# A fused four-layer decoder: values weighed ahead of the next unit's scores, and ones matmuls ahead of the last norm's transposes in the local blocks

## The chip, the cores and the metric

The kernel runs on one core of a Trainium2 chip. The metric is the time of one execution on the device in microseconds (us); lower is better. The engines are TensorE (PE in the profile, with its weight loads as PEld), VectorE (DVE), ScalarE (ACT), GpSimd (POOL) and SyncE (SP).

## The reference

A decoder of four layers, in float32, on x of 16 sequences x 64 tokens x 128 features, with a context of the same shape. Every layer has a self-attention or a recurrence, a cross attention and a feed-forward part, each with a residual and a layer norm after it. What this change touches lies in layer 0's third part, a small stack of two local-attention layers:

```python
for l in range(2):
    h = shift_token(x)                    # second half of the features from the token before
    q, k, v = split(h @ wqkv[l])          # 8 heads of 64
    q, k = rotary_xpos(l2norm(q) * qs, l2norm(k) * ks)
    attn = softmax(where(mask, -max, 8 * q @ k.T))     # causal, inside a window of 64 tokens
    x = x + (attn @ v) @ wo
    h = layer_norm(shift_token(x)) * lg + lb
    a, g = split(h @ w1 + b1)
    x = x + (a * gelu(g)) @ w2 + b2
x = layer_norm(x_before + x)
```

A sequence has 64 tokens, so a window is a sequence. What follows the stack is layer 1's self-attention (at1) and its cross attention (xa1).

## The kernel before, in words

The 1024 tokens are cut into two halves of 512, h = 0 and h = 1. Each half is a Python generator (`first_stream`) that emits one step of work up to each `yield`; `side_by_side` takes a step of half 0, then a step of half 1, and so on, with half 0 five steps ahead. Every engine carries out its instructions in the order that comes out of this, after a scheduler has moved some of them by a few places. [...]

`local_half(h)` emits the two local layers of one half. A half has two units u of 256 tokens, a unit two rows r of 128 tokens. One layer has these helpers:

- `rotate(u)`: the q and k products (lb_qk), their norms on ACT and DVE, and the rotary turn (lb_t; the sums on POOL).
- `values(u)`: the v products (lb_pv), copied to lb_v with a column of ones for the softmax sums.
- `flip(u)`: transposes of q and k (lb_pf, L868), copied to lb_qkT.
- `weights(u)`: 32 score matmuls, listed as 64 in the profile, into lb_sc (L880), two more for the mask (L889), the maximum (L901) and the subtraction (L902) on DVE, and Exp on ACT (L905), which gives lb_e.
- `turn(u)`: transposes of lb_e (lb_pt, L914), copied to lb_eT.
- `weigh(u)`: for each row 32 matmuls of lb_eT by lb_v into two PSUM tiles lb_av (L932), the reciprocal of the sum column (L942) and the product with it (L943, lb_ao). At the end of row 1 it calls `gather(u, 0)`.
- `gather(u, r)`: transposes of lb_ao (lb_pao, L957), copied to lb_oT (L958).
- `put(u)`: the output product (lb_po) and the residual (L972).

Then come the layer's norm (lb_hn), its transposes (lb_phn) behind six ones matmuls, the gated products (lb_pg, lb_pa, Gelu on ACT at L1045, the gating product on DVE at L1048), and the second product (lb_pw) with the residual (L1063 in layer 0, L1068 in layer 1). Layer 0 ends with transposes (lb_px) and their copies to lb_hs, which the next layer's lb_qk reads. Layer 1 ends in `close`, with the tag "lb": statistics on DVE, the inverse root on POOL, the normed xt_lb on DVE (L206). Its `flip`, called one step later, transposes xt_lb (px_lb, L224), and ACT copies that to x_lb, which at1's q and k products (at_pq, at_pk) read.

The order of the steps before the change, for each layer:

```python
            turn(0)
            flip(1)
            yield
            weights(1)
            weigh(0)
            yield
            turn(1)
            gather(0, 1)
            put(0)
```

With half 0 five steps ahead and eleven steps to a layer, `weights(1)` and `weigh(0)` of a half stand between the gated products of the other half and its lb_pw. In half 0's first layer they stand beside the end of half 1's first cross attention (xa_pao, po_xa, y_xa, px_xa).

`keep_busy` is one matmul of 128x128 ones by 128x512 ones in bfloat16 (L156, "ones"); its result is overwritten. at1 and the cross attentions place such matmuls in front of many of their products. `close` has a parameter `ones`, the number of them that its `flip` places ahead of the transposes; it is 0 unless given, and the local block gave none.

PSUM tiles of the pool `pt` (all of lb_pf, lb_pg, lb_pa, lb_pt, lb_av, lb_pao, lb_po, lb_pw and the like) rotate through four buffers: a tile waits for the readers of the tile four places earlier. lb_sc and lb_qk are of another pool with two. SBUF tiles of one size, lb_e, lb_eT, lb_oT and lb_t among them, rotate through seven buffers.

Of the kernel before, what the change touches and what calls it, by code (L numbers as in the profile page):

```python
# [37 lines left out]
class Kernel:  # L38
# [745 lines left out]
    def local_half(self, h):  # L784

        nc = self.nc
        work, psc, pt = self.aw, self.psc, self.pt
# [3 lines left out]
        for l in range(2):  # L791
# [64 lines left out]
            def flip(u):  # L856

                to = self.buf(8, [8, 256], f"{tag}_qkT{u}")
                both, rs = turned.pop(u)
                for r, t1 in enumerate(both):  # L860
                    t3 = t1.rearrange("p t (n d) -> p (t n) d", d=64)
                    nc.gpsimd.tensor_tensor(  # L862
                        t3, t3, rs[:, bass.ts(r, 16)].unsqueeze(2).to_broadcast([P, 16, 64]), ALU.mult
                    )
                    for t in range(2):
                        ps = pt.tile([P, 4, P], F32, tag="t", name=f"{tag}_pf{u}{r}{t}")
                        for c in range(4):
                            nc.tensor.transpose(ps[:, c, :], t1[:, t, bass.ts(c, P)], ident)  # L868
                        nc.scalar.copy(to[:, 4 * t : 4 * t + 4, bass.ts(r, P)], ps)
                qkT[u] = to  # L870

            def weights(u):
                sc = psc.tile([P, 2, HALF], F32, tag="sc", name=f"{tag}_sc{u}")
                for r in range(2):
                    for c in range(4):
                        for j in range(2):
                            for hh in range(2):
                                rows = slice(64 * hh, 64 * hh + 64)
                                t = slice(r * P + 64 * j, r * P + 64 * j + 64)
                                nc.tensor.matmul(  # L880
                                    sc[64 * j : 64 * j + 64, hh, bass.ts(r * 4 + c, S)],
                                    qkT[u][rows, c, t],
                                    qkT[u][rows, 4 + c, t],
                                    start=r == 0 and c == 0,
                                    stop=False,
                                    skip_group_check=True,
                                )
                for hh in range(2):
                    nc.tensor.matmul(  # L889
                        sc[:, hh, :],  # L890
                        self.ident_b,
                        self.causal_b.unsqueeze(1).to_broadcast([P, 8, S]),
                        start=False,
                        stop=True,
                        skip_group_check=True,
                    )
                e = self.buf(4, [2, 4, P], f"{tag}_e{u}")
                e3 = e.rearrange("p g n (a k) -> p (g n a) k", k=S)
                scored = sc.rearrange("p g (n k) -> p (g n) k", k=S)
                mx = work.tile([P, 16], F32, tag="mx", name=f"{tag}_mx{u}")  # L900
                nc.vector.tensor_reduce(mx, scored, AX.X, ALU.max)  # L901
                nc.vector.tensor_tensor(  # L902
                    e3, scored, mx.unsqueeze(2).to_broadcast([P, 16, S]), ALU.subtract
                )
                nc.scalar.activation(e3, e3, AF.Exp, scale=8.0)  # L905
                es[u] = e
# [11 lines left out]
            def weigh(u):  # L918


                eT = eTs.pop(u)
                oTs[u] = self.buf(4, [2, 4, P], f"{tag}_oT{u}")
                for r in range(2):
                    av = [
                        pt.tile([P, 4, 65], F32, tag="t", name=f"{tag}_av{u}{r}{cp}") for cp in range(2)
                    ]
                    for a in range(2):
                        for hh in range(2):
                            for j in range(2):
                                for cp in range(2):  # L930
                                    rows = slice(64 * cp, 64 * cp + 64)
                                    nc.tensor.matmul(  # L932
                                        av[cp][64 * j : 64 * j + 64, 2 * a + hh, :],
                                        eT[rows, hh, r * 2 + a, 64 * j : 64 * j + 64],
                                        v[rows, u * 4 + r * 2 + j, 2 * a + hh, :],
                                        start=True,
                                        stop=True,
                                    )
                    ao = self.buf(2, [2, 4, 64], f"{tag}_ao{u}{r}")
                    for cp in range(2):  # L940
                        rc = work.tile([P, 4], F32, tag="rc", name=f"{tag}_rc{u}{r}{cp}")
                        nc.vector.reciprocal(rc, av[cp][:, :, 64])  # L942
                        nc.vector.tensor_tensor(  # L943
                            ao[:, cp, :, :],
                            av[cp][:, :, 0:64],
                            rc.unsqueeze(2).to_broadcast([P, 4, 64]),
                            ALU.mult,
                        )
                    aos[u, r] = ao.rearrange("p c n d -> p (c n d)")
                    if r == 1:  # L950
                        gather(u, 0)

            def gather(u, r):
                flat = aos.pop((u, r))
                ps = pt.tile([P, 4, P], F32, tag="t", name=f"{tag}_pao{u}{r}")
                for n in range(4):
                    nc.tensor.transpose(ps[:, n, :], flat[:, bass.ts(n, P)], ident)  # L957
                nc.scalar.copy(oTs[u][:, r, :, :], ps)  # L958
# [29 lines left out]
            turn(0)  # L988
            flip(1)
            yield  # L990
            weights(1)
            weigh(0)
            yield
            turn(1)
            gather(0, 1)
# [65 lines left out]
            if l == 0:  # L1061
                x_in = self.buf(2, [4, D], f"{tag}_x2")
                nc.vector.tensor_tensor(x_in, ps, base, ALU.add)  # L1063
                self.shifted(self.psum(pt, f"{tag}_px"), h, x_in)
                yield
            else:
                y = self.new_y("lb", h)
                nc.vector.tensor_tensor(y, ps, base, ALU.add)  # L1068
                flip = self.close(pt, h, y, "lb")
                yield "last"  # L1070
                flip()

# [922 lines left out]
```

## Time and profile before

| | us |
|---|---|
| three runs | 893.00, 896.45, 899.19 |
| median | 896.45 |
| profiled execution | 892.14 |
| its span | 890.4 |
| PE busy | 737.5 (83%) |
| DVE busy | 493.2 (55%) |
| ACT busy | 361.7 (41%) |
| POOL busy | 264.8 (30%) |

The mean granted clock of PE in the profiled execution is 0.893 of full speed. The local blocks of the two halves lie between about 113 and 372 us of the span. [...] In a row of the timeline the columns are start, duration, engine, line, operation, what is written from what, shapes, count, and in brackets the idle time before it with what ended it. In a row of the chain they are start, duration, engine, tile and line. In a row for a stretch they are the bounds, the length, busy time and count of PE, PEld, DVE, ACT and POOL, the granted PE clock, the DMA share and GB/s.

### The profile page before, as it was taken

How to read it: one execution, taken by the hardware profiler on the slowest of the kernel's cores; microseconds unless marked ns; L12 is line 12 of the kernel's file. 1: busy time of each engine (PE TensorE's matmuls, PEld its weight loads, DVE VectorE, ACT ScalarE, POOL GpSimd, SP SyncE). 2: the span in 40 equal slices, each digit the busy share in tenths (PEclk: the TensorE clock that was granted, in tenths of full speed). 3: DMA queues.
4: the chain of work that ended last, by engine and by line, in shares of the span. 5: the costliest groups of instructions: out<-in, count | busy, mean ns of one | idle time of the engine just before them, and what ended most of it. 6: DMA issues, size and time to landing. Idle time of an engine off the chain costs nothing.

```text
span 890.4 us, 17664 instructions
## 1 busy us (share of the span) xinstructions
PE 737.5 (83%) x7145; PEld 467.7 (53%) x7147; DVE 493.2 (55%) x1126; ACT 361.7 (41%) x602; POOL 264.8 (30%) x299
## 2 busy tenths in 40 slices
PE   6777888878777889789978999869767999968990
PEld 2334546455554556457564577536444565735770
DVE  4565466564846656364536575445444456665663
ACT  2223456355455534364713365323215434512320
POOL 2323143260615321212025300146151011017732
PEclk7878989899999999899977899969968799968995
DMA  7700000000000000500000000152106632021102
GB/s 278 242 13 13 1 1 2 13 1 2 1 1 1 2 1 1 190 2 1 1 1 1 1 3 1 43 134 71 49 22 190 190 115 76 14 107 51 54 25 80
DMA packets 35543, 44.43 MB, mean 50 GB/s; under 512 B 7732, under 2 KB 27445, under 8 KB 34824
## 3 DMA queue, kind: packets, MB, share of 16 engines
q1 hardware_dynamic: 33000, 38.26, 13.6%
q0 software_dynamic: 2464, 5.05, 2.0%
q8 instruction: 58, 0.95, 0.4%
q14 instruction: 21, 0.17, 0.1%
HBM read 34.51 MB, written 11.80 MB: 52 GB/s over the span
## 4 chain that ended last, share of the span: by engine, by line
PE 54%; DVE 18%; POOL 7%; ACT 5%; issue 4%; DMA 3%; SPq 1%; DVEq 0%; POOLq 0%; ACTq 0%
PE xa_sc L480 4%; PE xa_av L572 4%; PE xa_pt L551 3%; PE tt_py L151 3%; PE sw_pe L151 3%; PE tt_ph L151 2%; PE at_sc L480 2%; DVE lb_t L818 2%; PE lb_qk L151 2%; DVE lb_t L832 2%; PE at_av L572 2%; PE xa_sc L491 2%; PE at_pt L551 2%; PE xa_pt L156 1%; PE lb_pw L151 1%
## 5 line engine op out<-in xcount | busy, mean ns | idle before, releaser
L536 DVE TENSOR_REDUCE xa_mx<-xa_sc 128x16 f32<-128x1024 f32 x40 | 48.7, 1219 | 63.8 <-PE xa_sc L491 41.3
L838 POOL TENSOR_TENSOR lb_t<-lb_t,lb_t 128x1024 f32<-128x1024 f32 x16 | 37.7, 2357 | 99.4 <-DVE lb_t L832 95.2
L554 ACT COPY xa_eT<-xa_pt 128x512 f32<-128x512 f32 x80 | 45.5, 587 | 40.8 <-PE xa_pt L551 40.0
L540 ACT ACTIVATE xa_e<-xa_e 128x1024 f32<-128x1024 f32 x40 | 42.3, 1058 | 37.6 <-DVE xa_e L537 37.5
L480 PE MATMUL xa_sc<-xa_km,xa_q 32*64 32x256 f32 x640 | 55.2, 404 | 0.7 <-ACT xa_q L431 0.5
L441 POOL TENSOR_SCALAR xa_km<-xa_k,const 128x512 f32<-128x512 f32 x40 | 27.0, 695 | 82.5 <-ACT xa_k L429 49.1
L551 PE MATMUL xa_pt<-const,xa_e 128*128 128x128 f32 x320 | 48.8, 280 | 1.8 <-ACT xa_e L540 1.8
L537 DVE TENSOR_TENSOR xa_e<-xa_sc,xa_mx 128x1024 f32<-128x1024 f32 x40 | 48.7, 1218 | 2.1
L551 PEld LDWEIGHTS xa_pt<-const,xa_e 128*128 128x128 f32 x320 | 40.3, 145 | 13.1 <-ACT xa_e L540 3.7
L572 PEld LDWEIGHTS xa_av<-v,xa_eT 128*64 128x64 f32 x1280 | 40.5, 138 | 8.2 <-issue 6.1
L572 PE MATMUL xa_av<-v,xa_eT 128*64 128x18 f32 (+1 forms) x1280 | 44.2, 209 | 0.0
L156 PEld LDWEIGHTS <-ones_b 128*128 128x128 bf16 x255 | 25.3, 106 | 35.9 <-issue 19.8
L151 PE MATMUL lb_qk<-w,lb_hs 128*128 128x512 f32 x64 | 35.8, 686 | 8.5 <-DVE lb_t L832 4.8
L480 PEld LDWEIGHTS xa_sc<-xa_km,xa_q 32*64 32x64 f32 x640 | 24.7, 136 | 19.9 <-issue 12.8
L201 POOL TENSOR_TENSOR rstd_xa<-mv_xa,eps 128x4 f32<-128x4 f32 x8 | 1.6, 200 | 112.2 <-DVE mv_xa L197 112.2
L814 DVE TENSOR_REDUCE lb_ss<-lb_t 128x16 f32<-128x1024 f32 x16 | 19.5, 1217 | 27.9 <-ACT lb_t L811 27.9
L156 PE MATMUL xa_pt<-ones_b 128*128 128x512 bf16 x80 | 30.2, 390 | 0.0
L862 POOL TENSOR_TENSOR lb_t<-lb_t,lb_rs 128x1024 f32<-128x1024 f32 x16 | 30.1, 1902 | 0.0
L1610 POOL DMA_INDIRECT tt_out<-tt_ys,tt_outs x23 | 22.5, 976 | 18.6 <-DVE tt_ys L1609 16.2
L868 PE MATMUL lb_pf<-const,lb_t 128*128 128x128 f32 x128 | 20.1, 312 | 9.4 <-POOL lb_t L862 9.3
L480 PE MATMUL at_sc<-at_km,at_q 32*64 32x256 f32 x256 | 22.5, 446 | 6.0 <-DVE at_rel L533 4.5
L151 PE MATMUL sw_pe<-sw_gu,sw_xs 128*128 x46 | 26.7, 665 | 0.0
(471 smaller groups left out, 1762.9 us busy)
## 6 DMA issues: line engine op xcount, KB each, us to landing
sw_gu<-in_sw_gu SPq DMA_DIRECT2D x4, 1024.0 KB, 6.8
at_mem<-at_rsb SPq DMA_DIRECT2D x16, 256.0 KB, 2.7
at_rel<-at_mem SPq DMA_DIRECT2D x32, 128.0 KB, 2.9
w<-in_w SPq DMA_DIRECT2D x1, 3114.0 KB, 13.7
sw_dn<-in_sw_dn SPq DMA_DIRECT2D x4, 512.0 KB, 7.0
tt_w<-in_tt_w SPq DMA_DIRECT2D x2, 1024.0 KB, 8.0
tt_b<-in_tt_b SPq DMA_DIRECT2D x1, 2048.0 KB, 7.4
sw_in<-in_zeros SPq DMA_DIRECT2D x1, 1472.0 KB, 11.2
```

What stands on the lines that cost most here:

```text
L151: self.nc.tensor.matmul(out, lhsT, rhs, start=n == 0, stop=n == len(pairs) - 1)
L156: self.nc.tensor.matmul(out, self.ones_b, self.ones_b.unsqueeze(1).to_broadcast([P, 4, P]), start=True, stop=True)
L441: nc.gpsimd.tensor_scalar(kms[-1][:, i % 4, :], k, hm[:, i : i + 1], 1.0, ALU.mult, ALU.mult)
L480: nc.tensor.matmul(sc[64 * j : 64 * j + 64, gg, at : at + 256], q[r, t], part[r, :, t] if local else part[r, :, :], start=not masked or (p ...
L536: nc.vector.tensor_reduce(mx, scored, AX.X, ALU.max)
L537: nc.vector.tensor_tensor(e3, scored, mx.unsqueeze(2).to_broadcast([P, 16, S]), ALU.subtract)
L540: nc.scalar.activation(e3, e3, AF.Exp, scale=scale)
L551: nc.tensor.transpose(ps[:, bass.ts(n, P)], blocks[:, bass.ts(n, P)], self.g("ident"))
L554: nc.scalar.copy(eT[:, gg, :], ps)
L572: nc.tensor.matmul(av[64 * j : 64 * j + 64, pr, hp, :, :], eT[:, gg, at : at + 64], v[:, b, hp, :, :], start=True, stop=True,)
L838: nc.gpsimd.tensor_tensor(t1, t1, t2.rearrange("p t n d -> p t (n d)"), ALU.add)
L862: nc.gpsimd.tensor_tensor(t3, t3, rs[:, bass.ts(r, 16)].unsqueeze(2).to_broadcast([P, 16, 64]), ALU.mult)
```

## The change

In each local layer `weigh(0)` is emitted ahead of `weights(1)`, within the same step. The close of the local block gets ones: 2 matmuls for half 0 and 7 for half 1, between the last lb_pw and the transposes px_lb.

```diff
             turn(0)
             flip(1)
             yield
+            weigh(0)
             weights(1)
-            weigh(0)
             yield
             turn(1)
             gather(0, 1)
@@
                 y = self.new_y("lb", h)
                 nc.vector.tensor_tensor(y, ps, base, ALU.add)
-                flip = self.close(pt, h, y, "lb")
+                flip = self.close(pt, h, y, "lb", ones=2 + 5 * h)
                 yield "last"
                 flip()
```

In the instruction order that results, PE has for each layer the lb_av matmuls, the four lb_pao transposes of row 0, and then the scores with the mask, where it had the scores first. DVE has the four reciprocals and four products ahead of the maximum and the subtraction. ACT has the copy lb_oT of row 0 ahead of the Exp. POOL and SP keep their order. Beside half 1's close the 7 ones stand behind the last at_av of half 0's attention, then the two ones of at_pq and at_pk, then the four px_lb transposes together, which were interleaved with those two ones.

## The prediction

> **What bounds the kernel now.** I read the page's shares first, then the chain of waits from 140 to 225 us and from 360 to 382, then the timeline of the same stretches with its releasers, and last the busy time and granted clock of single stretches. The page says that TensorE (PE) is 54% of the chain and that its clock is not full throughout:
>
> ```profile
> PE 54%; DVE 18%; POOL 7%; ACT 5%; issue 4%; DMA 3%; SPq 1%; DVEq 0%; POOLq 0%; ACTq 0%
> PEclk7878989899999999899977899969968799968995
> ```
>
> The reordered steps run four times: at about 149 us (call it A: half 0, layer 0, beside the end of half 1's first cross attention), 204 (B: half 1, layer 0), 256 (C: half 0, layer 1) and 310 (D: half 1, layer 1). B, in the chain of waits:
>
> ```profile
> 204.46 1.09 PE lb_sc L880 x64
> 205.55 0.55 PE lb_sc L889 x2
> 206.10 0.02 issue
> 206.13 1.23 DVE lb_mx L901
> 207.35 0.09 DVE lb_rc L942
> 207.44 1.17 DVE lb_e L902
> 208.61 0.33 DVE lb_ao L943
> ...
> 209.59 0.44 PE lb_pao L957 x2
> 210.04 2.69 PE lb_pw L151 x24
> ...
> 213.57 0.66 PE lb_px L235 x4
> 214.22 0.87 PE lb_pt L914 x8
> ```
>
> and in the timeline:
>
> ```profile
> 206.02 1.16 PE L932 MATMUL lb_av<-lb_v,lb_eT 64*64 64x65 f32 x64
> 208.69 1.28 ACT L905 ACT_TABLE_LOAD   x1 [4.37 <-DVE lb_e L902]
> 209.09 0.95 PE L957 MATMUL lb_pao<-const,lb_ao 128*128 128x128 f32 x4 [1.91 <-DVE lb_rc L942]
> ```
>
> The reader is to see that PE ends the value products at 207.18 and stands still until 209.09: their quotients (lb_ao) are queued on VectorE behind the maximum and the subtraction of the other unit's scores, and everything after on PE, the other half's lb_pw first, stands behind lb_pao. Also that ScalarE's table load for Exp waits for lb_e. C has the same rows 51.8 us later, D 105.9 later.
>
> The second edit is at half 1's close:
>
> ```profile
> 368.46 0.76 DVE xt_lb L206
> 369.26 0.47 PE px_lb L224
> 369.74 0.43 PE at_pq L156
> ...
> 371.91 2.07 PE at_pq L151 x2
> 373.98 1.72 PE at_pk L151 x2
> 365.60:369.20 3.60, 0.04 (x2) 0.00 (x0) 2.40 (x12) 0.00 (x0) 1.92 (x3) 0.95 0.94 292
> 369.00:375.60 6.60, 5.66 (x10) 2.22 (x10) 2.70 (x12) 1.17 (x2) 2.61 (x4) 0.50 0.98 361
> ```
>
> The last two lines are stretches: PE works 0.04 us of 3.6, and then has a clock of 0.50 for 6.6 us. Half 0's at_pq at 324.20, at full clock, takes 1.12 us for the same two matmuls.
>
> [...] the half clock comes in spells of 3.4 us or twice that (164.0 to 167.4, 369.0 to 375.6), behind idle stretches. [...] lb_ao waits behind lb_e with its operands long there. [...] the trace has 1283 ns for all six at L905.
>
> **The move, part by part.** It adds no work; PE, VectorE and ScalarE keep their instructions in another order, POOL and SP keep theirs. B, starting when lb_sc started (204.46):
> 1. The 64 lb_av matmuls (1.16) go first. Tiles rotate through four PSUM buffers, and the last of the four lb_av tiles takes the buffer that half 0's third gating multiplication (L1048, 204.57 to 205.32) reads. So the second 32 matmuls start at 205.36: end 205.9. This is the added wait; before, the scores covered it.
> 2. VectorE, nothing in front now: two reciprocals 0.20, two products 0.36 each (spacing at 175.86 to 176.66) from 205.32: 206.24. Last two lb_pao transposes: 206.5.
> 3. Scores and mask, 1.09 + 0.55: 208.14. lb_pw therefore starts at 208.14, not 210.04.
> 4. lb_pw 2.69, L1063 0.70, with 0.1 of hand-overs, lb_px 0.66: PE reaches lb_pt at 212.27, against 214.22.
> 5. The exponents must be there by then: maximum 1.23, subtraction 1.2, exponential 1.06 from 208.17 give 211.72. This holds only if the table load is out of the way. In the changed instruction stream ScalarE has the lb_oT copy, then the load without a wait, then the exponential with the wait for lb_e [...]. The load then runs from about 207.2 to 208.5, under the scores. If it still waited, lb_pt would start at 213.05.
> So B gives 1.95 us. lb_hs and the next lb_qk follow lb_px, so the whole front moves. C has the same figures: 1.95.
>
> D: lb_pw ends at 316.74 instead of about 318.6. But four ones matmuls (at_sc, 0.215 each) that sat in the stalls (313.02 and 314.58) now come behind lb_pw and push lb_pt to 317.65, against 318.46. lb_pt, lb_pao and lb_po (the copies of lb_eT and lb_oT beside them, as before) end at 321.05. half 0's norm, started by lb_pw, is done by 321.4. The two new ones cost 2 x 0.215: px_lb runs from 321.5 to 321.95. Before it ended at 323.53, paced by xt_lb. D gives 1.55 with the ones paid; they replace nothing that was cold, so I count them as cost alone.
>
> A: no table load. lb_av 148.9 to 150.0, products done at 150.7, scores to 152.6, xa_pao and po_xa to about 154.0. y_xa, with its first piece ahead of lb_e and three behind it, ends at 156.25 instead of 158.66; its norm ends at 159.85. lb_pt waits for exponents until 156.5, lb_po ends at 160.0, px_xa at 160.8 instead of 162.63: 1.85 us. But PE now idles 154.0 to 156.5, as it did from 151.65 to 153.6, which brought the half clock from 153.7 to 157.1. With a half clock on lb_pt, lb_pao and lb_po (3.5 us of work) A would lose up to 2.5 us instead. Before pays a like price; I take +1.3, bounds -2.5 and +2.
>
> **The ones at half 1.** Seven of 128x512 bf16, 0.215 each, stand behind at_av (end 365.7): 1.5 us, and the two of at_pq and at_pk follow, out from between the px_lb transposes: done at 367.7 at full clock, at 369.6 at half (9 x 0.43), 0.3 past the 369.26 at which xt_lb is there. If they hold the clock: px_lb ends after the last xt_lb (369.97) at 370.2 instead of 371.25 (1.0), at_pq 1.12 instead of 2.07 (0.95), at_pk 0.86 instead of 1.72 (0.86): 2.8 us, all on the chain that goes on to at_km and at_sc. If not, -0.4. Idle shrinks from 3.6 to 1.6 us; I take four chances in five, 2.3 us.
>
> **Sum.** 1.3 + 1.95 + 1.95 + 1.55 + 2.3 = 9.05 us. Later stages keep their order and move as a whole; the weight loads that start at 364.6 serve stages beyond 590, so they absorb nothing. The profiled execution took 892.14 (span 890.4): 883.1. The median of the runs shown is 896.45, 4.3 above it, which spells of half clock can explain; the same saving from it gives 887.4.
>
> **Rivals.**
> - The ones buy nothing, or A falls into a half clock (PE idles 2.5 us there): 9.05 less about 2.5 leaves 6.55: 889.9. For it: 1.6 us of idle is still ahead of px_lb. Against: B's 1.9 us of idle brought no half clock.
> - The table load stays behind lb_e, and the exponents take the place of the removed wait: B and C 1.2 each, D nothing (lb_pt at 318.9, px_lb at 323.2), A and the ones as above: 6.0 saved, 890.5. For it: the load waits so in all three places now. Against: the changed stream.
> - More than the sum: at B, C and D the old stalls, in executions whose windows fall otherwise, bring half clocks that now go. Full prices (10.1) and two spells of 1.7 us (half of 3.4): 883.0.
> - Slower: shifting the front moves all later work against the clock's windows. Place: the new idle in A, then the stages beyond 372 us, with gaps as long; price: 1.7 us of PE work for a spell. From six more spells the saving of 9.05 is gone; at seven the time is 899.3. Against it: B, C and D have less idle than before.
>
> **How the numbers follow.** Forecast 887.4 with 0.50; the first rival 0.15, the second 0.08, more 0.17, slower 0.10. The runs of before spread over 893.0 to 899.19, so each centre carries some 3 us. Low end: full prices and two spells, less 2: 881. High end: the poorer rivals and 4 of scatter: 894. About 1% (8.96 us, 887.5) is what can be told from no change: a little over half of the forecast (0.28), nearly all of "more" (0.17) and 0.05 of the first two rivals are faster, 0.50; slower by over 1% 0.04; the rest, 0.46, within.
>
> **What would show it.** At B and C: lb_av before lb_sc, lb_pw some 3.7 us after the start of lb_av, a table load at L905 that ends before lb_e does, lb_pt right behind lb_px. At D: px_lb without pacing. In A: lb_pt at full clock. At half 1's close: at_pq near 1.12 us. Wrong would be lb_pt waiting for lb_e at B, an at_pq still at 2 us, or the front at half 1's px_lb less than 5 us earlier.

## The result, and the profile after

| us | before | after |
|---|---|---|
| median (20 runs of each) | 894.20 | 887.17 |
| lowest, highest | 887.45, 902.00 | 882.21, 898.51 |
| profiled execution, its span | 892.14, 890.4 | 884.55, 882.8 |
| mean granted PE clock there | 0.893 | 0.902 |

The ratio is 0.9932, with a 95% interval of 0.9910 to 0.9953: 6.1 us less, between 4.2 and 8.0. (Executions more than 1.5% above the fastest of their kernel are left out of the ratios here, so these are not the quotients of the medians.) The forecast was 887.4. That it lies so close has some luck in it, told further down.

The page's shares of the chain and its row of clocks, as they are after:

```profile
PE 55%; DVE 17%; POOL 7%; ACT 5%; issue 4%; DMA 2%; SPq 1%; DVEq 0%; POOLq 0%; ACTq 0%
PEclk8877889999999798999987999969968999979995
```

VectorE has one per cent less of the chain and TensorE one more. The low digits of the clock are still there, at other places. Step B in the chain of waits (start, duration, engine, tile, line):

```profile
206.76 0.76 DVE lb_hid L1048
...
207.56 0.69 PE lb_av L932 x30
208.25 0.63 PE lb_pao L957 x4
208.88 1.09 PE lb_sc L880 x64
209.98 0.54 PE lb_sc L889 x2
210.51 2.69 PE lb_pw L151 x24
...
214.04 0.66 PE lb_px L235 x4
214.70 0.87 PE lb_pt L914 x8
```

and the rows of the timeline that answer to those of before:

```profile
206.59 0.79 PE L932 MATMUL lb_av<-lb_v,lb_eT 64*64 64x65 f32 x34
207.56 0.69 PE L932 MATMUL lb_av<-lb_v,lb_eT 64*64 64x65 f32 x30 [0.18 <-DVE lb_hid L1048]
209.58 1.28 ACT L905 ACT_TABLE_LOAD   x1
213.14 1.06 ACT L905 ACTIVATE lb_e<-lb_e 128x1024 f32<-128x1024 f32 x1 [2.28 <-DVE lb_e L902]
```

The maximum and the subtraction (L901, L902) are gone from the chain. PE goes from the value products through the transposes and the scores into lb_pw without standing still. The price is the first line: the second part of the value products is now released by the gating product on VectorE, and PE is idle for 0.18 us in front of it. The table load carries no wait. It ends at 210.86, and the Exp starts 2.28 us later, behind lb_e alone. lb_pt follows lb_px with no gap.

Half 1's close, in the chain:

```profile
368.37 0.75 DVE xt_lb L206
...
369.17 1.11 PE px_lb L224 x4
...
370.94 1.34 PE at_pq L151 x2
372.28 1.72 PE at_pk L151 x2
```

The ones no longer stand between the transposes. at_pq begins at full clock and ends at half; at_pk is at half clock throughout, 1.72 us as before.

The rest of the result does not lie in the steps that were edited. I cut the local blocks where one half's front passes from step to step, and took the length of each stretch from the traces. A begins with the first score or value matmul of the step, whichever comes first; "px_xa" and "lb_px" are the first of those transposes; the last entries run to the first at_pq of half 0 and, by way of px_lb, of half 1. Steps are in bold; sums are of the unrounded lengths. All kernels of the experiments are in the one table; the experiments say what each is.

| us | **A** to px_xa | to B | **B** to lb_px | to C | **C** to lb_px | to D | **D** to at_pq, half 0 | to px_lb, half 1 | **close** to at_pq, half 1 | sum |
|---|---|---|---|---|---|---|---|---|---|---|
| before | 12.7 | 42.9 | 9.2 | 42.6 | 9.2 | 45.0 | 13.9 | 45.1 | 2.6 | 223.0 |
| after | 11.7 | 41.8 | 7.5 | 43.7 | 7.5 | 46.6 | 12.7 | 44.7 | 1.8 | 217.9 |
| ones_only | 12.7 | 42.8 | 9.2 | 42.6 | 9.2 | 45.0 | 13.9 | 45.1 | 1.8 | 222.3 |
| copy_after_exp | 11.7 | 41.8 | 7.5 | 44.6 | 7.5 | 46.5 | 13.6 | 42.8 | 2.6 | 218.5 |
| before_phn12 | 12.7 | 42.8 | 9.2 | 42.6 | 9.2 | 45.0 | 13.9 | 46.0 | 2.6 | 224.0 |
| after_phn12 | 13.2 | 40.3 | 7.5 | 42.6 | 7.5 | 45.8 | 12.7 | 45.8 | 1.8 | 217.1 |
| dve_first_ones | 10.6 | 40.3 | 7.9 | 42.6 | 7.9 | 44.3 | 12.7 | 42.5 | 1.8 | 210.6 |
| dve_fill | 10.6 | 39.6 | 7.9 | 42.8 | 7.9 | 45.3 | 13.4 | 42.5 | 1.9 | 211.9 |
| shift14 | 15.9 | 41.8 | 7.5 | 43.6 | 7.5 | 46.6 | 12.7 | 44.7 | 1.8 | 222.0 |
| shift11 | 14.1 | 40.3 | 7.5 | 43.7 | 7.5 | 44.2 | 12.7 | 42.5 | 1.8 | 214.2 |

From before to after the bold columns gain 1.0, 1.7, 1.7, 1.2 and 0.9, in all 6.4 us up to the first at_pq. The stretches between them, whose instructions the change did not touch, give 1.1 and 0.4 and take 1.1 and 1.6: 1.2 us is lost there. Together that is 5.2; the half of at_pq that ran at full clock adds 0.7.

The two profiled executions are 7.6 us apart, so not all of that lies here. Ahead of A, where the change touches nothing, after took 4.2 us more than before (153.1 against 148.9); behind half 1's at_pq it took 6.6 less (511.9 against 518.5, with a mean clock of 0.90 against 0.88). So the local blocks can be compared to 0.1 us, as the experiments show, but the whole cannot: the rest of the program differs between executions by several us.

The lost time can be seen. In the stretch from B's lb_px to C the 16 transposes lb_pf of one unit stand in both chains; in that of before

```profile
249.20 1.81 PE lb_pf L868 x16
```

and in that of after

```profile
249.45 3.18 PE lb_pf L868 x16
```

The clock in these two traces is either full or half (1.00 or 0.50), and from its first change to its last every stretch at one of the two lasts a whole number of 3.413 us. In the local blocks a spell of half clock lasts one or two such lengths: 197.64 to 201.05 and 300.04 to 306.86 in after, 153.83 to 157.24 and 331.32 to 338.15 in before. One length is called a window here. Counted from the start of the span, the windows begin at 0.23 us and whole lengths later in before, at 3.08 in after.

The rows for stretches of after (bounds, length, busy time and count of PE, PEld, DVE, ACT and POOL, PE clock, DMA share, GB/s) show where the clock went:

```profile
245.41:248.82 3.41, 1.47 (x10) 1.07 (x11) 3.02 (x9) 1.46 (x3) 2.35 (x2) 1.00 0.00 0
248.82:252.23 3.41, 3.41 (x19) 3.41 (x18) 0.00 (x0) 2.80 (x6) 0.00 (x0) 0.50 0.00 0
```

against the same place in before:

```profile
242.49:245.91 3.42, 2.38 (x16) 0.88 (x12) 3.15 (x17) 2.95 (x4) 3.42 (x3) 1.00 0.02 5
245.91:249.32 3.41, 1.99 (x15) 1.59 (x16) 2.58 (x7) 1.45 (x3) 1.83 (x2) 1.00 0.00 0
```

PE waits there for the Exp on ACT (lb_e) and then for the norm on DVE (lb_hn) in both kernels. In before that wait is cut by a window boundary: PE is busy for 2.38 of 3.4 us on one side and 1.99 on the other, and the clock stays whole. After, most of the wait falls into one window, with 1.47 us of work, and the next window has half the clock, just when PE has all of its work there. At 300 us, in the stretch to D, before has one window of half clock and after two: lb_pf takes 3.41 us there instead of 2.39.

The stretch to B has such a spell too, at 197.6 (lb_pf 3.10 us instead of 1.81), and is still 1.1 us shorter after the change, because two spells of before are gone from it. The one at 164.1 had lain on the four lb_qk that follow px_xa:

```profile
163.88 3.64 PE lb_qk L151 x4
```

After, they take 2.00 us. From A on, before has seven spells and after six; what one costs depends on the work that it meets. The spell of before at 232.3, in the stretch to C, cost 0.46 us (four lb_pf, 1.13 instead of 0.67), the one of after at 248.8 cost 1.37. In A, before had a spell at 153.8 and after has none, so part of what A gained may be clock.

In these two kernels, from 112 us to half 1's at_pq, all ten windows at full clock with PE busy for up to 0.44 of their length (1.49 us) were followed by one at half clock. From 0.48 on one at full clock followed, except behind four windows: one of 0.59 in each kernel (ahead of the spells at 331.5 and 331), and in after one of 0.55 ahead of the spell at 371.7 and one of 0.54, from 112.3 us, ahead of the spell at 115.7. Others between 0.51 and 0.55 were followed by full ones (0.51 at 180.6 in after, 0.55 at 174.3 in before), so the border is not sharp.

### The profile page after: what moved, and what is told of

Its sections match the earlier page's. It is cut to its first block, busy times and chain, and to the rows that moved or that the text cites. A ratio compares the mean times of both kernels' runs of the same rounds, so it can differ in the third digit from the quotient of the medians.

```text
span 882.8 us, 17684 instructions
## 1 busy us (share of the span) xinstructions
PE 733.7 (83%) x7156; PEld 470.1 (53%) x7156; DVE 493.3 (56%) x1126; ACT 362.3 (41%) x602; POOL 265.1 (30%) x299
## 4 chain that ended last, share of the span: by engine, by line
PE 55%; DVE 17%; POOL 7%; ACT 5%; issue 4%; DMA 2%; SPq 1%; DVEq 0%; POOLq 0%; ACTq 0%
PE xa_sc L480 5%; PE xa_av L572 4%; PE xa_pt L551 4%; PE tt_py L151 3%; PE sw_pe L151 3%; PE tt_ph L151 2%; PE lb_pf L868 2%; PE xa_sc L491 2%; PE xa_pt L156 2%; PE at_av L572 2%; DVE lb_t L832 1%; PE lb_qk L151 1%; DVE lb_t L818 1%; PE at_pt L551 1%; PE at_sc L480 1%
## 5 line engine op out<-in xcount | busy, mean ns | idle before, releaser
L554 ACT COPY xa_eT<-xa_pt 128x512 f32<-128x512 f32 x80 | 45.4, 586 | 44.7 <-PE xa_pt L551 44.1
L151 PE MATMUL lb_qk<-w,lb_hs 128*128 128x512 f32 x64 | 33.4, 645 | 8.9 <-DVE lb_t L832 5.2
L868 PE MATMUL lb_pf<-const,lb_t 128*128 128x128 f32 x128 | 22.0, 334 | 10.5 <-POOL lb_t L862 8.6
L1590 ACT ACTIVATE tt_hid<-tt_hid 128x512 f32<-128x512 f32 x23 | 14.5, 630 | 29.5 <-DVE tt_hid L1589 29.5
L1333 POOL DMA_INDIRECT sw_got<-sw_in,sw_ids x23 | 22.1, 962 | 14.9 <-DVE sw_ids L1313 6.1
```

Of the source, the lines that this page charges most:

```text
L151: self.nc.tensor.matmul(out, lhsT, rhs, start=n == 0, stop=n == len(pairs) - 1)
L554: nc.scalar.copy(eT[:, gg, :], ps)
```

## The experiments

My theory after this reading had two parts. First, the steps save what their waits were worth. Second, the front, when it is moved by less than a window, falls otherwise into the clock's windows, and the spells of half clock that come or go decide what of the saving is left. The rivals were that the ones bring the gain, that it is the table load that moved, and that the stretches differ by chance from one execution to the next. Each kernel was compared with runs of before on the same chip. The chips differ (medians of before 893.8 to 909.3), so ratios and lengths are compared and not times.

### The two parts by themselves

move_only takes the ones out of after:

```diff
-                flip = self.close(pt, h, y, "lb", ones=2 + 5 * h)
+                flip = self.close(pt, h, y, "lb")
```

> The reordering alone, without the new ones. My theory, a stall taken out of VectorE's queue: at B and C lb_pw starts about 3.8 us after the first value matmul (5.58 from the first score matmul before), lb_pt about 8.0 us after it, and the whole is 6 to 7 us faster than before, ratio 0.993. Rival, most of what the two edits gain together is the clock that the ones hold up: then this alone gains 2 to 3 us, ratio 0.997, although the stall is gone.

Measured: 0.9970 (0.9942 to 0.9998), 22 runs. Of 908.54 us that is 2.7 us saved, at most 5.3; the four steps of the prediction sum to 6.75. The theory's 6 to 7 us missed, and the ratio is the one that the rival gave. The profiled execution was one of the slowest (916.39 us), so its stretches are not used.

ones_only has the ones without the move:

```diff
-                flip = self.close(pt, h, y, "lb")
+                flip = self.close(pt, h, y, "lb", ones=2 + 5 * h)
```

> The ones alone, in the order of before. My theory: half 1's at_pq and at_pk gain 1 to 2 us from a later half clock, half 0 pays 0.4 us; together 1 to 1.5 us, ratio 0.998 to 1.000, hardly to be told from nothing. Rival, the clock carries the gain: 4 us or more, ratio 0.995. Third possibility, the ones only cost their own 9 x 0.215 = 1.9 us: ratio 1.002.

Measured: 0.9985 (0.9966 to 1.0004), 22 runs: 1.4 us, not told from nothing. In the trace only the close moves, from 2.6 to 1.8, and all other lengths stay within 0.1. So the ones do what they do at one place, and the gain is not theirs alone; the rival, that the clock they hold up carries the gain (0.995), falls by this trace and by the interval. In time the two parts multiply to 0.9955, just outside after's interval, but their own intervals are too wide to say that they do not add up. Why the move alone saved so little is not shown.

### The table load

copy_after_exp is the move without ones, with the copy of row 0's lb_oT emitted after `weights(1)`, so that on ScalarE it stands behind the Exp:

```diff
-                nc.scalar.copy(oTs[u][:, r, :, :], ps)
+                late.append((oTs[u][:, r, :, :], ps))
+                if u == 1 or r == 1:
+                    nc.scalar.copy(*late.pop())
...
             weigh(0)
             weights(1)
+            nc.scalar.copy(*late.pop())
```

> The reordering alone, with one change on ScalarE: the copy lb_oT of the first unit's row 0 comes behind the Exp instead of ahead of it. The Exp's table load then stands right behind the Gelu and carries the wait for lb_e, as before the change. If the load matters as the prediction said (rival two there), lb_pt waits for the exponents: at B and C it starts about 8.6 to 8.8 us after the first value matmul instead of 8.0, at D some 1.2 us later, in all 2 to 3 us slower than the reordering alone, ratio 0.996. If the load is hidden anyhow: as the reordering alone, 0.993.

At B, its timeline

```profile
213.62 1.28 ACT L905 ACT_TABLE_LOAD   x1 [3.55 <-DVE lb_e L902]
```

and its chain:

```profile
212.31 1.24 DVE lb_e L902
...
213.62 1.28 ACT L905
...
214.91 1.06 ACT lb_e L905
...
216.02 1.09 PE lb_pt L914 x8
```

The load waits for lb_e again, and lb_pt comes 8.9 us after the first value matmul instead of 8.1. It is on the chain at B; the stretch behind B, to C, is 0.9 us longer than in after, and so is D, which has 0.43 us of ones less. The stretch behind C is not longer. So the place of the copy decides: with a plain copy between Gelu and Exp the load runs right behind the copy (209.58 in after, where the copy ends at 209.56) and carries no wait. The prediction had the load right. The rotation of buffers does not free the load by itself: this kernel takes its buffers in the same order as after.

In time nothing of it is to be seen: 0.9973 (0.9949 to 0.9997), 22 runs, against 0.9970 of move_only. The table shows why it may be so: the stretch to half 1's px_lb is 42.8 instead of 44.7, without the spell that after has there at 331. What the load costs at two places is given back at a third.

### Is it chance from run to run?

after_again is the changed kernel as it stands, in another set of runs.

> The changed kernel once more, beside the next three on the same chip. Ratio to before 0.993, as measured first (0.991 to 0.9953). If the two parts measured alone add up instead (0.997 and 0.9985), 0.9955.

Measured: 0.9859 (0.9804 to 0.9913), 6 runs, lower than both of the expected ratios. Its total of 217.8 and its nine lengths are those of after, none further off than 0.1 us; ahead of A it took 154.3 us, and behind half 1's at_pq 515.4. So the stretches are no scatter, and the better ratio does not come from them. They belong to the kernel, although A began 1.2 us later in it than in after (154.3 against 153.1). Why they come again was not shown.

### Where a spell comes, and whether filling takes it away

after_phn12 puts twelve ones instead of six ahead of the norm's transposes lb_phn, which lie in the window before the lb_pf that ran at half clock; before_phn12 is its control.

```diff
-            for _ in range(6):
+            for _ in range(12):
                 self.keep_busy(ps)
```

> The changed kernel with 12 ones matmuls instead of 6 ahead of each layer's lb_phn transposes. Theory: part of the move's saving is given back by half clocks. In the changed kernel's trace all three layers that run beside a lb_phn wait (198, 249, 300 us) have lb_pf at half clock, because the 3.4 us window before holds only 1.4 us of PE work; at 1.7 us and more no half clock came. Six more ones (1.3 us) inside the wait fill that window: lb_pf takes 2.0 us instead of 3.1 to 3.6, and the whole is 2 to 4 us faster than the changed kernel, ratio 0.989. Rival, chance of the windows' position: the spells come somewhere else and the time stays at 0.993, or the ones delay the transposes and it is 0.995.

> Control: the kernel before with 12 ones ahead of lb_phn instead of 6. In its trace one of the three waits was followed by a half clock. Theory: 1 to 2 us faster than before, ratio 0.998 to 0.999. If the ones there are worth the same in both kernels: 0.996 and the theory of a saving given back in the changed kernel alone falls.

Measured: 0.9911 (0.9882 to 0.9940), 22 runs, for after_phn12, and 1.0020 (0.9995 to 1.0045), 14 runs, for the control. The stretch to C is 42.6 instead of 43.7 and that to B 40.3 instead of 41.8, as expected. The third spell stayed (295.8; lb_pf 3.17 us). A is 1.5 us longer, with a spell at 156, and the stretch to px_lb 1.1, with others at 227.5, 278.5 and 323. The sum is 217.1 against 217.9 of after, so 0.8 us where 2 to 4 were expected: two spells went where they were filled, and others came elsewhere. In the control two of the three windows were whole before, the third spell stayed (299.5), and the ones cost 0.9 us in one stretch; the 1 to 2 us expected of it did not come.

Three kernels shift after's front by ones ahead of half 1's px_xa, where PE waits anyway for the norm, and change nothing else:

```diff
         ones = 8 if h == 1 and tag in ("xa2", "xa3") else 1
+        if h == 1 and tag == "xa0":
+            ones += 14          # shift14; 4 in shift4, 11 in shift11
```

> The changed kernel with 14 more ones matmuls (3.0 us of PE time at full clock) ahead of px_xa, at the end of half 1's first cross attention; they delay everything after them. Theory: in the changed kernel the front stands so in the 3.413 us windows that the ones and the wait ahead of lb_phn fall into different windows, and the window of the wait holds under 0.45 of PE work in each of three layers, which gives 5 us or so back between the steps. 3.0 us later is the same as 0.4 us earlier by the window, so the half clocks on lb_pf at 198, 249 and 300 us go: the stretch from px_xa to at1's at_pq of half 0, 159.7 us in the changed kernel, takes 159.7 + 3.0 - 3 to 5, so 158 to 160, in spite of the added work, and the whole is within 2 us of the changed kernel (ratio 0.990 to 0.994). Rival, position of the windows does not matter: 162.7 us and 3.0 us slower (0.993 to 0.996).

> The changed kernel with 4 more ones (0.86 us) at the same place. Theory: by the window this is 0.86 us later, the wait ahead of lb_phn still fills a window of its own with less than 0.45 of PE work, the half clocks stay, and the stretch from px_xa to half 0's at_pq is 160.5 us or more; ratio to before about 1 us worse than the changed kernel's. Rival: the same 160.5, from the delay alone. Both agree here; with the run of 14 it shows whether the delay or the position counts.

> The changed kernel with 11 more ones (2.37 us) ahead of px_xa. In the changed kernel px_xa stood 1.3 us behind a window's boundary and the stretches to B, C and D took 41.8, 43.7 and 46.6 us; in the run with scores first on TensorE and quotients first on VectorE it stood 0.2 us behind one and they took 40.3, 42.6 and 44.2. 2.37 us later puts the changed kernel at 0.25 behind the next boundary. If the position by the window decides, the stretches become 40.3, 42.6 and 44.2 or near, and from the first value matmul of A to half 0's at_pq it takes 171.4 + 2.4 - 5 = 169 us, less than without the added work; the whole 2 to 3 us faster than the changed kernel, ratio 0.988. If the order of the steps itself makes the stretches, they stay at 41.8, 43.7, 46.6: 173.8 us, ratio 0.995. If the profiled execution enters A at another position than the changed kernel's did, the stretches are to be read against the position that px_xa then has.

Measured: shift14 0.9956 (0.9928 to 0.9983), 15 runs; shift4 0.9899 (0.9861 to 0.9936), 15 runs; shift11 0.9920 (0.9890 to 0.9950), 22 runs. shift14 took more than its 3.0 us: its A is 4.2 longer, with a spell of its own at 160. px_xa then lay near the place in a window where it lies in after (1.3 us behind a boundary), and the other lengths are those of after to 0.1 us: the half clocks that were to go came again, and the ratio is what the delay alone was to give. It told nothing of another position, then, but it shows that a front 4.2 us later met the same lengths. shift11 came to another position: px_xa stands some 0.4 us behind a boundary. Its A is 2.4 us longer, as the 11 ones cost, and three stretches, to B, D and px_lb, are 1.5, 2.4 and 2.2 us shorter. The one to C is as long as in after, with a spell at 248.8; 42.6 us had been expected. Its rows at 197.6, where after has 1.37 us of work in the first window and a clock of 0.51 in the second:

```profile
194.20:197.60 3.40, 2.08 (x14) 0.66 (x10) 3.07 (x16) 3.09 (x4) 3.40 (x3) 1.00 0.00 0
197.60:201.00 3.40, 2.26 (x18) 1.87 (x19) 2.35 (x5) 1.45 (x3) 1.55 (x2) 1.00 0.01 2
```

The wait is cut in two again, 2.08 and 2.26 us of work, and the clock is whole. With 2.4 us of work added and nothing taken away, half 1's at_pq comes 214.2 us after the start of A instead of 217.9. That rules out the mere amount of work. Chance is unlikely, since the lengths of after came again in after_again and in shift14, but shift11 was traced once. In the total it cannot be told from after (0.9920 against 0.9932, where 0.988 was expected); what the stages beyond 372 us make of a front that comes at another time was not followed. Of shift4 the ratio is as weak as the spread of its runs (877.69 to 895.45 us, median 889.62, which is 0.9953 of before's). In its profiled execution, 892.24 us long, px_xa to half 0's at_pq took 157.5 us, where 160.5 or more had been expected. From one execution nothing is concluded.

### Another order with the same aim

If VectorE's queue is the cause, the scores need not move. dve_first leaves before's order on PE, and asks for the maximum and the subtraction behind the products:

```diff
+            def exps(u):        # maximum, subtraction and Exp, cut out of weights(u)
...
             weights(1)
             weigh(0)
+            exps(1)
             yield
```

`weights(0)` is followed at once by `exps(0)`. dve_first_ones has the ones at the close as well.

> TensorE keeps the order of before (scores ahead of values), only VectorE changes: the four reciprocals and products of the first unit come ahead of the second unit's maximum and subtraction. If the stall is one of VectorE's queue, lb_pw starts about 3.7 us after the first score matmul at B and C, and the whole is within 1.5 us of the reordering alone (ratio 0.993 to 0.995; the maximum starts some 0.4 us later than there). If TensorE's order is what counts, nothing is gained: ratio 1.000, lb_pw 5.6 us after.

> Scores ahead of values on TensorE, quotients of the first unit ahead of the second unit's maximum on VectorE, and the changed kernel's ones at the close (2 and 7). That order alone showed 0.984 in few runs. Theory A, that order is as good as the move or better by 1 to 2 us because no PE wait for the fourth lb_av buffer is added: 0.991 with the ones. Theory B, it is far better because the front falls differently into the clock's windows: 0.984 to 0.986 again. If the few runs misled: 0.993 as the changed kernel.

Measured: dve_first 0.9841 (0.9782 to 0.9900), dve_first_ones 0.9825 (0.9788 to 0.9863), 6 runs each. The first is a weak number: its runs lie between 888.66 and 910.02 us, and their median of 902.13 is 0.9929 of before's. The second is what theory B gave. B of dve_first_ones in the chain:

```profile
203.66 1.09 PE lb_sc L880 x64
...
205.33 1.22 DVE lb_mx L905
...
206.71 0.40 DVE lb_ao L947
...
207.93 2.69 PE lb_pw L151 x24
```

The scheduler still lets the maximum go first, and only the subtraction comes behind the products (at 208.28 in the timeline). lb_pw starts 4.27 us after the first matmul of the step; in before that was 5.58, in after 3.92. So the step saves less than in after, 7.9 against 7.5 in the table. Still the sum is 7.3 us shorter than after's: 0.8 is lost in B and C, 1.1 gained in A, and 1.5, 1.1, 2.3 and 2.2 in the four stretches between. From A on it has two spells of half clock, at 231 and 282.5; after has six, at 197.5, 249, 286.5, 300, 331 and 371.7. On the chip that ran both, the medians are 878.60 for dve_first_ones and 884.48 for after_again; their intervals overlap (0.9788 to 0.9863, 0.9804 to 0.9913), so in the total it is the best kernel of the study, but not shown to beat after.

dve_fill puts six ones ahead of the first lb_pf of dve_first_ones, to fill the windows before the two spells that are left:

```diff
+                        if (u, r, t) == (0, 0, 0):
+                            for _ in range(6):
+                                self.keep_busy(ps)
```

> Scores first on TensorE, first unit's quotients first on VectorE, the ones at the close (2 and 7), and 6 ones more ahead of the first transposes of each unit 0's flip, where PE waits for the products on GpSimd. In that order's trace two half clocks are left in the local blocks, at 231 and 282 us, both behind this wait (windows busy 0.39 and 0.32). Theory: they go, 2 to 3 us faster than without the fill: ratio 0.980. Rival: other windows empty instead, or the ones sit ahead of the wait and fill the wrong window: 0.983, no difference.

Measured: 0.9847 (0.9815 to 0.9880), 6 runs. The spells at 231 and 282.5 went, and three came at 241, 292.5 and 360.5, the last two of two windows each. The local blocks are 1.3 us longer. The expectation missed.

## Why the prediction was right or wrong

**B and C.** Right in kind and in size. lb_pw starts 3.92 us after the first value matmul (predicted 3.68), lb_pt 8.11 (7.81), where before had 9.76. The added wait for the fourth lb_av buffer is there, 0.18 us in front of the second part at 207.56; I had the second part start 0.90 after the first, and it was 0.97. B and C give 1.7 each, for 1.95. The load costs its 1.28 us and no more where it is on the chain: in copy_after_exp the Exp starts 0.01 us after it.

**D.** 1.2 for 1.55. The four ones behind lb_pw and the two new ones are there. lb_pt had to wait for the exponents until 7.66 us after the start, where I had 7.28 from the ones alone.

**A.** 1.0 to px_xa's start, 1.4 to its end, for 1.3 (1.85 without a half clock), and the half clock that the range held in reserve did not come there. In after_phn12 and shift14, where it did, it cost 1.5 and 1.2 us: the bound of 2.5 was wide.

**The ones at half 1.** 1.6 for 2.3 (from xt_lb to at_km 6.34 instead of 7.94 us). px_lb and the first half of at_pq gained as worked out. The 2.3 was also a little high by its own odds: four in five of 2.8, less one in five of 0.4, is 2.2. The step that failed is that the clock holds up to at_pk: PE is idle for 1.57 us ahead of px_lb and 0.68 behind it, and the window from 368.3 to 371.7, with 0.87 us of the one and all of the other in it, 1.88 of 3.41 us busy, was followed by the spell at 371.7.

**The whole front moves.** This was the wrong step. It moves only between spells. Of 9.05 us, the steps to at_pk delivered about 7.2 (A 1.0, B 1.7, C 1.7, D 1.2, ones 1.6), and 1.2 of that went in the stretches between: 5.9 us from A's start to the end of at_pk (226.8 before, 220.9 after). One of the prediction's own signs of being wrong came with it, the front at half 1's px_lb less than 5 us earlier: counted from the start of A it is 4.3 us earlier (216.1 against 220.4). The fourth rival, "slower", named this mechanism, but put it into A and beyond 372 us and asked for six more spells. Inside the local blocks four spells of before went and three came at other places, one of the rest grew by a window and one shrank by one.

**The base.** The forecast set the saving of 9.05 against a median of three runs, 896.45. Over twenty runs it is 894.20, 2.25 lower. The saving was some 2 us too large by the medians (7.0), the base 2.25 too high, and the two cancelled. What the prediction earned is the sign, the size to a third (9.05 for 6.1 by the ratio), and the mechanism at the four steps; not the last tenth of a microsecond.

**The rivals.** The load behind lb_e is refuted in after's trace, and copy_after_exp shows what it would have cost at a place. "The ones buy nothing" is refuted at their place by ones_only's trace, though not by its ratio; the half clock in A, its other branch, did not come. That windows fall otherwise in other executions of before was an estimate of that rival and was not shown; "more than the sum" did not come with this kernel, but dve_first_ones shows that it can: its steps save 0.4 us less than after's at B and at C, and its local blocks are 12.5 us shorter than before's.

**Open.** Why the ratio of after is 0.9932 in one set of runs and 0.9859 in the other, with intervals that barely touch (0.9910 and 0.9913 are the ends that meet), while the local blocks in the two traces are alike; what the windows do ahead of A and beyond 372 us; and an order whose spells are all gone, which neither way of filling reached.

## What to carry to other kernels

When the quotients of one unit and the maximum of the next share an engine, put first what the other engines wait for: here it was worth 1.7 us at each of two places, and the chain of waits showed it as a busy engine in front of an idle one (PE idle for 1.91 us). Work out the saving step by step, but don't move the rest of the program by it as a block: where PE waits often and shortly, part of the saving can be taken back, as 1.2 of 6.4 us were here, with waits that no longer straddled two windows of 3.41 us. Compare the lengths of untouched stretches first; where they differ, look at the clock in the rows for stretches before any other cause, and try a second order with the same aim, since the one that saves less in its own step can save more over the stretches between: here 7.3 us more in the local blocks, though the total was not shown to differ.

## What the runs showed of the hardware

- In the local blocks of before and after every spell of half clock lasted one or two windows of 3.413 us. All ten windows at full clock with PE busy for up to 0.44 of them were followed by a half one; above that four were, at 0.54, 0.55 and twice 0.59.
- The lengths of the steps and of the stretches between them repeated to 0.1 us in another execution (after_again) and, from px_xa on, in shift14, which ran on another chip than after_again; and with 2.4 us of added matmuls (shift11) the local blocks were 3.6 us shorter.
- The table load directly behind the Gelu waited for the Exp's operand (idle 4.37 us in before, 3.55 in copy_after_exp, both at B); with a plain copy between Gelu and Exp (after) it ran 0.02 us behind the copy, 3.6 us ahead of the Exp, and was not on the chain.
